# Bilinear bias in a deformable-attention kernel: left columns weighted by diagonal matrices on TensorE, and the right columns of one block in eight with them

## The chip, the cores and the metric

One Trainium2 chip, one of its cores. The metric is the device time of one execution in microseconds (us); three executions of the kernel before were timed. A profile of one more execution shows when each instruction ran on each engine: TensorE (PE), VectorE (DVE), ScalarE (ACT), GpSimd (POOL) and SyncE (SP, which issues DMAs).

## The reference, cut to what matters

Two layers: a deformable attention over 4 images of 32x32 pixels with 384 channels and 6 heads, then a linear attention and a mixture of four experts. The change lies in the first layer, where each head adds a bias to the attention logits. The bias of key n at all queries is a 32x32 window of a table, sampled bilinearly at an offset that belongs to that key:

```python
attn = jnp.einsum('bmhc,bnhc->bhmn', qh, k) * scale
disp = (ref.reshape(1, n, 1, 2) - pos.reshape(Bq * G, 1, n, 2)) * 0.5
...
bias = _bilinear_sample(rpe_img, disp)   # top = tl + ax*(tr - tl), bot likewise; top + ay*(bot - top)
...
attn = jax.nn.softmax(attn + bias, axis=-1)
out = jnp.einsum('bhmn,bnhc->bmhc', attn, v).reshape(Bq, Hq, Wq, NC)
return out @ w_out + b_out
```

## The kernel before, in words

The kernel has stages one after the other: normalisation, query projection, convolution, sampling of the keys and values (to about 400 us in the profile), the attention (to about 1395 us), the linear attention, and the experts. All data is float32. The attention stage is the one that the change touches.

Its loops run over 24 units (4 images x 6 heads) of 1024 keys and 1024 queries. A unit's keys are cut into 8 blocks of 128; two blocks make a pair `p`, so there are 96 pairs, and pair `p` is number `kp = p % 4` of its unit. Keys lie on the partitions, queries along the free axis. `e` (0 or 1) is the block within its pair.

For each block the bias is made in four steps with four weights per key, one number per partition (`weight(p, e, i)`, i = 0 to 3):
- `fetch_windows` (L1168): POOL fetches a 33x33 window of the table for each key by an indirect DMA into `win` (4 buffers).
- `upper` (L1184, ACT): rows 0 to 31 of the window times weight 0, into the tile `t` of 32x33 per key (4 buffers).
- `lower` (L1194, DVE): rows 1 to 32 times weight 1, added to `t`.
- `left` (L1202, ACT): columns 0 to 31 of `t` times weight 2, into the tile `o` of 32x32 per key (2 buffers). PE adds it to the logits in PSUM by a product with the identity (L1226, in `scores`).
- `right` (L1252, DVE): columns 1 to 32 of `t` times weight 3, plus the logits from PSUM, into the tile `S` in SBUF (6 buffers).

`scores(p, step)` makes the logits of a pair in the PSUM tile `ps`, of which there is one buffer (four banks of eight). PE's array is used as four quadrants of 64x64. In `step` 0 the products of queries and keys (L1221) go to the crossed quadrants for block 1, and the identity products of `o` (L1226) to the diagonal quadrants for block 0; in `step` 1 the blocks are exchanged. Each step has four products of each kind, each with 512 columns. Between the two steps PE waits for a small copy on ACT (`turn_over`, L1241).

After `right`, DVE keeps a running maximum over the pairs of a unit (`running`, L1270 and L1272). At the end of the unit PE transposes it (`highest`, L1282), DVE reduces it (L1286), and PE spreads the result (`spread`, L1298), which ACT copies (L1306). One unit later DVE subtracts it (`minus`, L1311), ACT takes the exponential (`weights_of`, L1315), and PE multiplies with the values (`values`, L1329 with the values and L1338 with ones). `out_of`, `to_queries` and `to_channels` (L1354 to L1412) finish a head, and `project` (L1429 to L1442) projects a finished image, 128 rows at a time. In the first units, where no image is finished, `last_pieces` runs what is left of the key and value projections of the stage before (helpers at L257 to L299).

The order on PE, ACT, DVE and POOL is that of the source. The loop at L1521 makes one turn per pair; turn `g` works on the scores of pair `g + 1` and on windows of pair `g + 2`, and finishes pairs four and five back:

```python
values(g - 5, 0)
scores(g + 1, 0)
for e in range(2):
    upper(g + 2, e)
...                                  # running(g), turn_over(g + 1), values(g - 5, 1), minus, weights_of
scores(g + 1, 1)
...                                  # highest, last_pieces(0), project(0)
for e in range(2):
    if kp:
        lower(g + 2, e)
    left(g + 2, e)
fetch_windows(g + 4)
right(g + 1)
```

Here `kp` is that of `g`, so the pair with number 3 is scored in the turn with `kp` = 2, and the maximum that takes it in stands in the turn with `kp` = 3, as does `highest`. `project` and `last_pieces` put their products behind `scores(g + 1, 1)` in turns with even `kp`.

Before the loop, L1504 to L1520 bring the first pairs in: four window fetches, `upper`, `lower`, `left`, `scores(0, ...)` and `right(0)`. The stage before ends with gathers of the sampled image (L871, POOL, six to a tile `ga`) that DVE weighs and adds (L886, L890, L891). Its PE, ACT, DVE and POOL work and that of the new stage share the engines' queues in one order, which follows when a tile's memory becomes free as well as the source.

Of the kernel before, what the change touches and what calls it, by code (L numbers as in the profile page):

```python
# [11 lines left out]
F32 = mybir.dt.float32  # L12
I32 = mybir.dt.int32
AF = mybir.ActivationFunctionType
# [5 lines left out]
P = 128  # L20
B, HI, WI, NC = 4, 32, 32, 384
# [3 lines left out]
G, GC = 6, 64  # L25
# [126 lines left out]
def bc(ap, axis, n):  # L152

    dims = [list(d) for d in ap.ap]
    dims.insert(axis, [0, n])
    return bass.AP(ap.tensor, ap.offset, dims)
# [3 lines left out]
def body(  # L160
# [8 lines left out]
    nc = tc.nc  # L169
# [11 lines left out]
    ident = const.tile([P, P], F32, tag="ident", name="ident")  # L181
# [60 lines left out]
    x0 = early.tile([P, NB, NC], F32, tag="x0", name="xr0")  # L242
# [58 lines left out]
    with tc.tile_pool(name="a_w", bufs=1) as aw, tc.tile_pool(name="a_1", bufs=1) as a1, tc.tile_pool(  # L301
        name="a_2", bufs=2
    ) as a2, tc.tile_pool(name="a_3", bufs=2) as a3, tc.tile_pool(name="a_s", bufs=2) as asm, tc.tile_pool(
        name="a_cv", bufs=1, space=PSUM
    ) as pcv, tc.tile_pool(name="a_mm", bufs=2, space=PSUM) as pmm, tc.tile_pool(
        name="a_tr", bufs=3, space=PSUM
# [13 lines left out]
        step = plan.step  # L320
# [379 lines left out]
        os_ = {}  # L700
# [222 lines left out]
        for b in range(B):  # L923
# [56 lines left out]
            for f in range(2):  # L980
# [22 lines left out]
                for i, n in enumerate(sizes):  # L1003
                    k0, r = K4 * f + i * n, n / K4
# [109 lines left out]

    with tc.tile_pool(name="b_w", bufs=1) as bwp, tc.tile_pool(name="b_qkv", bufs=2) as bq, tc.tile_pool(
        name="b_win", bufs=4
    ) as bwin, tc.tile_pool(name="b_t", bufs=4) as bt, tc.tile_pool(name="b_o", bufs=2) as bo_, tc.tile_pool(
        name="b_s", bufs=6
    ) as bS, tc.tile_pool(name="b_m", bufs=2) as bm, tc.tile_pool(name="b_ao", bufs=1) as bao, tc.tile_pool(
        name="b_y", bufs=3  # L1120
# [2 lines left out]
        nc.sync.dma_start(wo, w_out.rearrange("(a p) d -> p a d", p=P))  # L1123
        bo = bwp.tile([P, NC], F32, tag="bo", name="bo")
        nc.sync.dma_start(bo, bc(b_out, 0, P))
        units = [(b, h) for b in range(B) for h in range(G)]
        ao = {}
        heads = {}

        HALF = [slice(e * GC, (e + 1) * GC) for e in range(2)]  # L1130
        FULL = [slice(f * 512, (f + 1) * 512) for f in range(2)]
        SYNC = mybir.DependencyInfo(mybir.DependencyClass.Sync, mybir.DependencyReason.DATA)
        KP = NB // 2
        NP = KP * len(units)

        def load_qk(u):


            b, h = u
            c, r0 = h // 2, (h % 2) * GC  # L1140
            q = bq.tile([P, N], F32, tag="q", name=f"q{b}_{h}")
            k = bq.tile([P, NB, GC], F32, tag="k", name=f"k{b}_{h}")
            ks = k_d[b][c][r0 : r0 + GC, :].rearrange("p (a e j) -> p a e j", e=2, j=GC)
            for e in range(2):
                nc.sync.dma_start(q[HALF[e], :], q_d[b][c][r0 : r0 + GC, :])
                nc.sync.dma_start(k[HALF[e]], ks[:, :, 1 - e, :])
            return q, k
# [9 lines left out]


        wins, ts, os_, pss, Ss, turns = {}, {}, {}, {}, {}, {}
        qk, vs, ms, nms, pbss, pos, avs = {}, {}, {}, {}, {}, {}, {}  # L1160

        def fetch_windows(p):
# [13 lines left out]
        def weight(p, e, i):  # L1176
            b, h = units[p // KP]
            return bw[b][:, 2 * (p % KP) + e, h, i : i + 1]
# [19 lines left out]
        def left(p, e):  # L1198

            if p < NP:  # L1200
                o = bo_.tile([P, HI, WI], F32, tag="o", name=f"o{p}_{e}")
                nc.scalar.activation(o, ts[p, e][:, :, 0:WI], AF.Copy, scale=weight(p, e, 2))  # L1202
                os_[p, e] = o.rearrange("p y x -> p (y x)")

        def scores(p, step):


            if p >= NP:
                return
            i, kp = divmod(p, KP)  # L1210
            if step == 0:
                if kp == 0:
                    qk[i] = load_qk(units[i])
                pss[p] = bps.tile([P, 2, N], F32, tag="s", name=f"ps{p}")
            q, k = qk[i]
            ps = pss[p]
            e, d = 1 - step, step
            made = []
            for f in range(2):
                for r in range(2):  # L1220
                    made.append(nc.tensor.matmul(  # L1221
                        ps[HALF[1 - r], e, FULL[f]], k[HALF[r], 2 * kp + e, :], q[HALF[r], FULL[f]],
                        start=(step == 0), stop=(step == 1),
                    ))
                for r in range(2):
                    made.append(nc.tensor.matmul(  # L1226
                        ps[HALF[r], d, FULL[f]], ident[HALF[r], HALF[r]], os_[p, d][HALF[r], FULL[f]],
                        start=(step == 0), stop=(step == 1),
                    ))
            if step == 0:  # L1230
                turns[p] = made
            else:
                for i_ in made:
                    tc.add_manual_dep(i_.ins, turns[p].ins.name, SYNC, reason="second quarters")
                del turns[p]
# [10 lines left out]
        def right(p):  # L1246

            if p < NP:
                ps = pss.pop(p)
                st = bS.tile([P, 2, N], F32, tag="S", name=f"S{p}")  # L1250
                for e in range(2):
                    nc.vector.scalar_tensor_tensor(  # L1252
                        st[:, e, :].rearrange("p (y x) -> p y x", x=WI),
                        ts.pop((p, e))[:, :, 1:WIN],
                        weight(p, e, 3),
                        ps[:, e, :].rearrange("p (y x) -> p y x", x=WI),
                        ALU.mult,
                        ALU.add,
                    )
                    del os_[p, e]  # L1260
                Ss[p] = st
# [236 lines left out]
        with tc.manual_schedule(  # L1498
# [9 lines left out]
            for p in range(2):  # L1508
                for e in range(2):
                    upper(p, e)  # L1510
                    lower(p, e)
                    if p == 0:
                        left(p, e)
                fetch_windows(p + 2)
            scores(0, 0)
            turn_over(0)
            scores(0, 1)
            for e in range(2):
                left(1, e)
            right(0)  # L1520
            for g in range(NP + 7):  # L1521


                i, kp = divmod(g, KP)
# [4 lines that stand above are left out]
# [30 lines left out]
# [5 lines that stand above are left out]
                if kp % 2 == 0:  # L1564
                    project(1)
                right(g + 1)
                if g == 15 * KP:
                    load_early()
# [7 lines left out]
            while waiting:  # L1576
                tag, n = spots.pop(0)
# [152 lines left out]
    with tc.tile_pool(name="c_1", bufs=1) as c1, tc.tile_pool(name="c_2", bufs=2) as c2, tc.tile_pool(  # L1730
        name="c_s", bufs=2
# [320 lines left out]
    with tc.tile_pool(name="d_w1", bufs=1) as dw1, tc.tile_pool(name="d_s1", bufs=1) as ds1, tc.tile_pool(  # L2052
        name="d_w2", bufs=1
    ) as dw2, tc.tile_pool(name="d_s2", bufs=1) as ds2, tc.tile_pool(name="d_2", bufs=2) as d2p, tc.tile_pool(
        name="d_h", bufs=3
# [94 lines left out]
        for t in range(-2, len(units)):  # L2150
# [12 lines left out]
            d = ds[j]  # L2163
# [59 lines left out]
```

## Time and profile before

| | us |
|---|---|
| three runs | 2848.89, 2853.29, 2854.21 (median 2853.29) |
| the profiled execution | 2848.2 |
| its span | 2846.1 |
| PE busy, of the span | 2586.8 (91%) |
| DVE | 1579.4 (55%) |
| ACT | 1157.8 (41%) |
| POOL | 855.1 (30%) |
| mean granted TensorE clock | 0.968 of full speed |

| line, engine | count | mean us | busy us |
|---|---|---|---|
| L1226 PE, left columns by the identity | 1536 passes | 0.612 | 378.4 |
| L1221 PE, queries by keys | 1536 passes | 0.611 | 382.1 |
| L1184 ACT, `upper` | 192 | 1.168 | 218.1 |
| L1202 ACT, `left` | 192 | 1.144 | 212.8 |
| L1194 DVE, `lower` | 192 | 1.316 | 244.7 |
| L1252 DVE, `right` | 192 | 1.277 | 237.1 |
| L1306 ACT, copy of 128x1024 from PSUM | 24 | 0.993 | 23.8 |

How to read it: a busy share is an average over stages with different limits. One float32 product shows as two passes on PE, and passes in different quadrants run at the same time, so their durations overlap and their sum is no time on PE. In a list in order of time the columns are the start and the duration in us, the engine, the line, the operation, what is written and read, the shapes (partitions x elements) and the count; a bracket gives the idle time of the engine just before and what ended it.

### The profile page before, as it was taken

What the parts mean: (1) busy time and instruction counts of PE and PEld (TensorE: products, weight loads), DVE (VectorE), ACT (ScalarE), POOL (GpSimd) and SP (SyncE); (2) the same over time, 40 slices, a digit from 0 to 9 for tenths busy, and PEclk for the clock granted to TensorE, in tenths of its full rate; (3) what the DMA queues carried; (4) which work ended last, traced back from release to release, by engine and by line L of the source; (5) the groups of instructions that cost most, each with busy time, mean ns of one, the idle gap of its engine ahead of it and who ended that gap; (6) DMA issues with size and microseconds to landing.
All of it is one profiled execution on the core that took longest, in us unless ns stands there. A gap on an engine that the chain in (4) does not pass through costs nothing. (4 is left out here: it accounts for less than half of the span.)

```text
span 2846.1 us, 33342 instructions
## 1 busy us (share of the span) xinstructions
PE 2586.8 (91%) x12731; PEld 1283.8 (45%) x12731; DVE 1579.4 (55%) x2349; ACT 1157.8 (41%) x1532; POOL 855.1 (30%) x776
## 2 busy tenths in 40 slices
PE   8899938898989988888799898999999999999999
PEld 5455512332333333233365554555555555555566
DVE  3888859999999999999656765000101011011011
ACT  5565536777667766676323322111111111111121
POOL 1668863232333333332112335211112111021121
PEclk9899969999999999999999999999999999999999
DMA  7934575454546555544121312622223433374371
GB/s 205 257 114 132 175 208 165 130 154 146 164 145 195 176 157 149 145 151 127 55 74 51 120 45 70 250 103 103 103 103 118 147 129 140 115 255 172 117 267 59
DMA packets 267899, 404.77 MB, mean 142 GB/s; under 512 B 134674, under 2 KB 207634, under 8 KB 267356
## 3 DMA queue, kind: packets, MB, share of 16 engines
q1 hardware_dynamic: 214912, 230.43, 25.6%
q0 software_dynamic: 52112, 172.15, 18.7%
q8 instruction: 100, 1.64, 0.2%
q14 instruction: 59, 0.48, 0.1%
q10 hardware_dynamic: 716, 0.07, 0.0%
HBM read 345.68 MB, written 70.06 MB: 146 GB/s over the span
## 5 line engine op out<-in xcount | busy, mean ns | idle before, releaser
L2070 PE MATMUL ph<-d_xT,w 128*128 128x512 f32 (+1 forms) x1152 | 484.1, 554 | 1.3 <-ACT h L2077 1.3
L2102 PE MATMUL acc<-w,h 128*128 128x384 f32 x1392 | 480.3, 486 | 0.0
L1168 POOL DMA_INDIRECT win<-table,widx x192 | 280.2, 1459 | 640.3 <-DVE t L1194 608.5
L1221 PE MATMUL ps<-q,k 64*64 64x512 f32 x1536 | 382.1, 611 | 90.7 <-DVE S L1252 43.6
L2077 ACT ACTIVATE h<-ph,b1c 128x512 f32<-128x512 f32 (+1 forms) x192 | 124.1, 647 | 776.3 <-PE ph L2070 761.7
L1226 PE MATMUL ps<-o,ident 64*64 64x512 f32 x1536 | 378.4, 612 | 9.5 <-ACT o L1202 9.5
L2102 PEld LDWEIGHTS acc<-w,h 128*128 128x128 f32 x1392 | 264.1, 190 | 208.5 <-issue 73.2
L2070 PEld LDWEIGHTS ph<-d_xT,w 128*128 128x128 f32 x1152 | 217.0, 191 | 196.3 <-issue 144.5
L2132 POOL DMA_INDIRECT out<-rows,ei x67 | 67.1, 1002 | 700.2 <-DVE rows L2129 691.4
L871 POOL DMA_INDIRECT ga<-img,pidx x192 | 233.5, 1216 | 145.7 <-DVE gd L600 62.5
L1315 ACT ACTIVATE S<-S 128x2048 f32<-128x2048 f32 x96 | 183.4, 1910 | 190.3 <-DVE S L1311 190.3
L1221 PEld LDWEIGHTS ps<-q,k 64*64 64x64 f32 x1536 | 99.2, 134 | 355.4 <-issue 211.5
L1722 DVE COPY d_xT<-e_tr 128x512 f32<-128x512 f32 (+2 forms) x75 | 36.6, 512 | 386.1 <-PE e_tr L1719 386.1
L1194 DVE SCALAR_TENSOR_TENSOR t<-win,bw,t 128x1056 f32<-128x1056 f32 x192 | 244.7, 1316 | 5.9 <-ACT t L1184 4.6
L1252 DVE SCALAR_TENSOR_TENSOR S<-t,bw,ps 128x1024 f32<-128x1024 f32 x192 | 237.1, 1277 | 18.9 <-PE ps L1226 16.0
L2121 DVE SCALAR_TENSOR_TENSOR rows<-b2r,en,rows 128x384 f32<-128x384 f32 x67 | 40.9, 618 | 359.9 <-DMA rows<-out,ei 321.1
L1184 ACT ACTIVATE t<-win,bw 128x1056 f32<-128x1056 f32 x192 | 218.1, 1168 | 39.2 <-DMA win<-table,widx 38.1
L1202 ACT ACTIVATE o<-t,bw 128x1024 f32<-128x1024 f32 x192 | 212.8, 1144 | 37.0 <-DVE t L1194 30.1
L1329 PE MATMUL po<-S,v 128*64 128x512 f32 x768 | 199.1, 642 | 24.4 <-ACT av L1354 13.9
L1311 DVE TENSOR_TENSOR S<-S,pbs 128x2048 f32<-128x2048 f32 x96 | 219.0, 2283 | 2.1 <-ACT pbs L1306 2.1
L2129 DVE SCALAR_TENSOR_TENSOR rows<-acc,en,rows 128x384 f32<-128x384 f32 x67 | 41.4, 618 | 218.2 <-PE acc L2102 216.3
L1270 DVE TENSOR_TENSOR m<-m,S 128x2048 f32<-128x2048 f32 x48 | 117.1, 2440 | 1.6
(350 smaller groups left out, 3442.0 us busy)
## 6 DMA issues: line engine op xcount, KB each, us to landing
w<-in_L_ffn_w SPq DMA_DIRECT2D x50, 2304.0 KB
img<-in_x SPq DMA_DIRECT2D x48, 256.0 KB
q<-q_d SPq DMA_DIRECT2D x48, 256.0 KB
x<-in_x SPq DMA_DIRECT2D x8, 768.0 KB
q_d<-qt SPq DMA_DIRECT2D x24, 256.0 KB
v_d<-qkvw SPq DMA_DIRECT2D x32, 192.0 KB
v<-v_d SPq DMA_DIRECT2D x24, 256.0 KB
k<-k_d SPq DMA_DIRECT2D x48, 128.0 KB
```

The lines of the kernel that those rows point to most:

```text
L871: nc.gpsimd.indirect_dma_start(out=ga[:, g].rearrange("p s c -> p (s c)"), out_offset=None, in_=img[b][:, :], in_offset=bass.IndirectOffse ...
L1168: nc.gpsimd.indirect_dma_start(out=win, out_offset=None, in_=tables[h // 2][:, :], in_offset=bass.IndirectOffsetOnAxis(ap=widx[b][:, nb, h ...
L1184: nc.scalar.activation(t.rearrange("p y x -> p (y x)"), wins[p, e][:, : HI * WIN], AF.Copy, scale=weight(p, e, 0),)
L1194: nc.vector.scalar_tensor_tensor(tf, wins.pop((p, e))[:, WIN:], weight(p, e, 1), tf, ALU.mult, ALU.add)
L1202: nc.scalar.activation(o, ts[p, e][:, :, 0:WI], AF.Copy, scale=weight(p, e, 2))
L1221: made.append(nc.tensor.matmul(ps[HALF[1 - r], e, FULL[f]], k[HALF[r], 2 * kp + e, :], q[HALF[r], FULL[f]], start=(step == 0), stop=(step ...
L1226: made.append(nc.tensor.matmul(ps[HALF[r], d, FULL[f]], ident[HALF[r], HALF[r]], os_[p, d][HALF[r], FULL[f]], start=(step == 0), stop=(ste ...
L1252: nc.vector.scalar_tensor_tensor(st[:, e, :].rearrange("p (y x) -> p y x", x=WI), ts.pop((p, e))[:, :, 1:WIN], weight(p, e, 3), ps[:, e, : ...
L1311: nc.vector.tensor_tensor(Ss[p], Ss[p], bc(pbss[p // KP][:, :], 1, 2), ALU.add)
L1329: nc.tensor.matmul(pos[i][0][HALF[f], :], vs[i][:, 2 * kp + e, :], Ss[p][:, e, FULL[f]], start=(first and e == 0), stop=(last and e == 1),)
L2070: nc.tensor.matmul(ph if short(d) else ph[:, :n], a, m, start=(c == 0), stop=(c == CK - 1))
L2102: nc.tensor.matmul(d["acc"][0 if short(d) else s][:, :NC], h[:, s * P : (s + 1) * P], d["w2"][:, hc, :], start=(hc == 0), stop=(hc == HC - 1),
```

## The change

ACT no longer weighs the left columns of a block. It writes a diagonal instead: `fold` is a tile of two 64x64 identities one above the other, and `diagonal` multiplies it by the weight of each key, which gives a 128x64 tile. `scores` multiplies this tile with the columns of `t` themselves, read by rows of 32 out of 33, in the place of the product of the identity with `o`. The tile `o` is 64 wide and has 6 buffers in the place of 2. For one block in eight (pair 3 of each unit, block 1) a second diagonal is made from weight 3, `scores` adds the right columns in the same way behind the left ones, and `right` copies the finished logits of that block from PSUM to `S` on ACT in the place of the pass on DVE.

```diff
-    ) as bwin, tc.tile_pool(name="b_t", bufs=4) as bt, tc.tile_pool(name="b_o", bufs=2) as bo_, tc.tile_pool(
+    ) as bwin, tc.tile_pool(name="b_t", bufs=4) as bt, tc.tile_pool(name="b_o", bufs=6) as bo_, tc.tile_pool(
...
+        fold = bwp.tile([P, GC], F32, tag="fold", name="fold")
+        for e in range(2):
+            nc.gpsimd.tensor_copy(
+                fold[e * GC : (e + 1) * GC, :], ident[e * GC : (e + 1) * GC, e * GC : (e + 1) * GC]
+            )
...
+        WHOLE, rights = ((3, 1),), {}
...
             if p < NP:
-                o = bo_.tile([P, HI, WI], F32, tag="o", name=f"o{p}_{e}")
-                nc.scalar.activation(o, ts[p, e][:, :, 0:WI], AF.Copy, scale=weight(p, e, 2))
-                os_[p, e] = o.rearrange("p y x -> p (y x)")
+                os_[p, e] = diagonal(p, e, 2)
+                if (p % KP, e) in WHOLE:
+                    rights[p, e] = diagonal(p, e, 3)
+
+        def diagonal(p, e, i):
+            o = bo_.tile([P, GC], F32, tag="o", name=f"o{p}_{e}_{i}")
+            nc.scalar.activation(o, fold, AF.Copy, scale=weight(p, e, i))
+            return o
+
+        def columns_of(p, e, r, f, x0):
+
+            return ts[p, e][HALF[r], 16 * f : 16 * f + 16, x0 : x0 + WI]
...
                 for r in range(2):
                     made.append(nc.tensor.matmul(
-                        ps[HALF[r], d, FULL[f]], ident[HALF[r], HALF[r]], os_[p, d][HALF[r], FULL[f]],
-                        start=(step == 0), stop=(step == 1),
+                        ps[HALF[r], d, FULL[f]], os_[p, d][HALF[r], :], columns_of(p, d, r, f, 0),
+                        start=(step == 0), stop=(step == 1 and (p, d) not in rights),
+                    ))
+                for r in range(2 if (p, d) in rights else 0):
+                    made.append(nc.tensor.matmul(
+                        ps[HALF[r], d, FULL[f]], rights[p, d][HALF[r], :], columns_of(p, d, r, f, 1),
+                        start=False, stop=(step == 1),
                     ))
...
                 for e in range(2):
+                    if rights.pop((p, e), None) is not None:
+                        nc.scalar.copy(st[:, e, :], ps[:, e, :])
+                        del os_[p, e], ts[p, e]
+                        continue
                     nc.vector.scalar_tensor_tensor(
```

## The prediction

> **What bounds the kernel now.** I read the row of 40 slices first, then busy times over a stretch of the attention stage, then the groups of that stretch, then its instructions in order of time. The stage runs from about 400 to 1395 us. VectorE (DVE) is full there from the seventh slice to the nineteenth, and TensorE (PE) close to it. Over 900 us in the middle (columns: length, then busy us of PE, weight loads, DVE, ACT, POOL, the granted clock, DMA):
>
> ```profile
> PE   8899938898989988888799898999999999999999
> DVE  3888859999999999999656765000101011011011
> ...
> 440.00:1340.00 900.00, 791.80 (x5228) 282.16 (x5224) 872.53 (x623) 632.65 (x634) 284.98 (x202) 0.98 0.52 155
> ```
>
> DVE is busy 872.5 of 900 us (97%), PE 88%, ACT 70%; the clock was 0.98. An average does not say whether PE could take more, so I looked at the turn that the change loads. A unit (one image, one head) has four turns; the block pair with kp = 3 is scored in the turn kp = 2. Unit 9, and then unit 10, from that point on:
>
> ```profile
> 797.10 2.20 PE L1429 MATMUL y<-wo,ao 128*128 128x384 f32 x6
> 798.66 2.47 DVE L1252 SCALAR_TENSOR_TENSOR S<-t,bw,ps 128x1024 f32<-128x1024 f32 x2
> 799.24 1.94 PE L1329 MATMUL po<-S,v 128*64 128x512 f32 x8
> 801.16 2.82 DVE L1270 TENSOR_TENSOR m<-m,S 128x2048 f32<-128x2048 f32 x1
> 801.23 0.74 PE L1221 MATMUL ps<-q,k 64*64 64x512 f32 x2
> ...
> 806.10 1.09 PE L1282 MATMUL pm<-ident,m 128*128 128x128 f32 x8
> 807.82 1.22 DVE L1286 TENSOR_REDUCE nm<-pm 128x8 f32<-128x1024 f32 x1
> ```
>
> ```profile
> 836.02 2.20 PE L1429 MATMUL y<-wo,ao 128*128 128x384 f32 x6
> 838.49 1.94 PE L1329 MATMUL po<-S,v 128*64 128x512 f32 x8 [0.26 <-ACT S L1315]
> 838.86 2.47 DVE L1252 SCALAR_TENSOR_TENSOR S<-t,bw,ps 128x1024 f32<-128x1024 f32 x2
> ...
> 841.43 0.74 PE L1221 MATMUL ps<-q,k 64*64 64x512 f32 x2 [1.01 <-issue]
> 846.30 1.09 PE L1282 MATMUL pm<-ident,m 128*128 128x128 f32 x8
> 848.04 1.22 DVE L1286 TENSOR_REDUCE nm<-pm 128x8 f32<-128x1024 f32 x1
> ```
>
> In unit 9 the scores end at 797.17 (the last L1221/L1226 pair starts at 796.58 and takes 0.6), and PE then runs without a hole: projection, values to 801.18, the next scores at 801.23. DVE's pass over the old scores ended at 801.13, so both engines arrive together. Six us later DVE's reduction L1286 needs the transposes L1282, and they end at 807.19, 0.63 before it. In unit 10 PE has 0.26 + 1.01 us of holes before the next scores, then 0.65. The reduction is where the two meet: everything DVE does next stands behind it, so what it moves by is what the unit moves by.
>
> **The change part by part.** All sums are against the profiled execution: 2848.2 us, 2846.1 of it span. That lies 3.9 below the mean of the three runs (2852.1) and 5.1 below their median, 2853.29.
>
> *Left columns.* ACT's L1202 (192 × 1.144 = 219.6 us by its mean, 212.8 busy) becomes a 128x64 pass. Nothing of that size is in the trace; the nearest are L800's 128x48 at 0.24 and the token copy's 128x1 at 0.19, so 0.25, and bounds 0.19 to 0.47 (L295, 128x384). ACT is 70% busy and its waits there are for DVE, as these lines of the stretch 440 to 1340 show (busy, mean ns, idle before and its releaser):
>
> ```profile
> L1202 ACT ACTIVATE o<-t,bw 128x1024 f32<-128x1024 f32 x178 | 197.0, 1143 | 27.9 <-DVE t L1194 24.7
> L1306 ACT COPY pbs<-pb 128x1024 f32<-128x1024 f32 x23 | 22.8, 992 | 0.0
> ```
>
> What ACT issues next (L1184) waits for the tile that DVE's L1252 frees, so the saving ends as ACT idleness: 0. PE does the same count of 64x64 matmuls for the left columns, with rows of 32 out of 33. The convolution's L713 reads 32 of 34 and takes 0.375 for 256 columns against 0.589 for 512: 0.214 for 256 columns, the rate of plain rows. So 0 there too; if strided rows cost more, 1536 passes would pay it, but no row speaks for it.
>
> *Right columns of 24 blocks (p % 4 = 3, e = 1).* PE gets four more matmuls a block, each two passes in the trace (L1226: 1536 rows for 768 matmuls). They use the same two quadrants as the left ones, and passes in one quadrant follow at 0.43 (804.22, 804.70, 805.13, 805.56). The half-step's diagonal quadrants go from 4 passes to 8: +4 × 0.4275 = 1.71 us. Bounds: 0.86, if half of them slip into the stretch in which the other two quadrants work, and 1.95, a whole half-step. I take 1.71, because two passes of one quadrant have never overlapped in the trace. DVE loses one of its two passes: 2.47 becomes 1.28. ACT gets a copy from PSUM of the same shape as L1306: 0.99.
>
> *A new wait.* In the built program that copy waits for VectorE's instruction on the first half of the same tile, not for PE. So the two run one after the other: 1.28 + 0.03 (ACT's start after a DVE end at 401.41) + 0.99 + 0.10 (DVE after ACT at 399.99) = 2.40 against 2.47 + 0.03. Behind the copy, DVE's L1270 needs the tile and PE's next scores need the PSUM buffer, which has no second copy. DVE's 24 × 1.28 = 30.7 us thus come back as waiting, all but 0.1 a unit.
>
> *What 1.71 us more on PE do to each unit*, by the ends in the trace (hole of PE before the next scores, and gap between L1282's end and L1286):
> - Units 1, 3, 5, 11, 12: a late piece (L270, L286) and values fill PE, holes 0, gap 0.04: +1.71 each, 8.55.
> - Units 0 and 4: holes 0.2 to 0.3: +1.42 each, 2.84. Units 2 and 6: hole 1.0: +0.65 each, 1.3.
> - Units 7, 9, 13, 15, 19, 21: projection, and the transposes L1405 of an odd head before the half-step, holes 0 to 0.1, gap 0.63 to 0.66: 1.71 less 0.65, +1.0 to 1.1 each, 6.15.
> - Units 8, 10, 14, 16, 20, 22, also 18 and 23: holes and gap of 1.9 or more swallow it; −0.1 each, −0.8. Unit 17: +0.2.
>
> Sum +18.2. Of the delay nothing is won back: after the reduction DVE has no hole up to the next unit that it could close.
>
> *The start of the stage.* The order of the built program moves more than the diff shows. Three of the first four window fetches (L1168) now stand ahead of the last 24 gathers (L871) on POOL, and ACT's first L1184 ahead of key and value copies, so ACT and, behind it, DVE stop until the first window lands.
>
> ```profile
> 393.36 1.97 POOL L1168 DMA_INDIRECT win<-table,widx  x1 [0.30 <-issue]
> 402.64 1.12 PE L1226 MATMUL ps<-o,ident 64*64 64x512 f32 x2 [9.52 <-ACT o L1202]
> 412.07 2.47 DVE L1252 SCALAR_TENSOR_TENSOR S<-t,bw,ps 128x1024 f32<-128x1024 f32 x2 [2.23 <-PE ps L1226]
> ```
>
> The three fetches took 393.36 to 399.69 = 6.3, so the gathers' last data, in use at 396.8, come at 403.1. The small matrix `fold` waits for them on POOL, the diagonals for `fold`: 403.4. ACT's next L1184 ends at 404.9, and DVE then has in its order the leftovers of the sampling (0.96 + 0.61, twice, and 1.76) and three L1194 (1.32): 8.9, so the first L1252 starts at 413.8 and not at 412.07: +1.7. SP's loads of keys stand behind ACT's late copies: ACT's stop runs from 345.6 to 366.6 (a fetch issued at 360 lands 5.4 later, L1184 1.17), so the copies that ended at 360.7 end near 379; keys landed at 391.2 and land near 402.4, hidden, because PE waits for the diagonals until 403.7. Bounds −2 (the wait for PE at 412.07 gone) and +6.3 (the fetches in full). `fold` itself, two 64x64 copies, lies in this.
>
> Total: +18.2 + 1.7 = +19.9, so 2868.1 by the profiled execution, and 2872 with the 3.9 by which the runs' mean lies higher.
>
> A page speaks against my reading of PE: the Trainium skill, Perfetto Trace Analysis, section Identifying the Most-Contended Engine, says that matmul busy time is no good measure of TensorE's headroom and that the share of weight loads is. Weight loads are 31% of the stretch above, by which PE would have room for the four matmuls, their price would be 0 and the sum far lower. The rows of unit 9, where the next scores follow the values with no hole, do not agree, and I go by them.
>
> **Rivals.**
> - *Half price on PE* (0.86): units 1, 3, 5, 11, 12 +4.3, 0 and 4 +1.1, the six odd ones +1.2, the rest −1.1: +5.5 + 1.7 = 7.2, so 2859. For it: four quadrants do run at once. Against: left and right share a quadrant.
> - *Faster*: the copy runs beside DVE's first half after all, and the four matmuls are free. Then the nine units on whose path PE already stands gain 0, the six odd ones their gap of 0.65, the nine others 1.19: −14.6 + 1.7 = −12.9, so 2839. It decides only where PE's price is under some 0.3 a block and the wait named above is not as built. For it: DVE at 97%. Against: both rows and the program.
> - *The start costs all it can*: 18.2 + 6.3 = 24.5, so 2877; or more, if the gathers fall behind the key loads on the DMA queues, which are busiest there. For it: an ACT stop of 21 us. Against: PE had 9.52 us of waiting there to give.
>
> **How the numbers follow.** Forecast 0.64, start dearer 0.14, half price 0.14, faster 0.06, nothing measurable from other causes 0.02. Predicted 2872. The range goes from a little under the half-price case, 2853 (start at −2, rest as there), to 2885: 1.95 a block adds 0.24 × 15 units = 3.6, start +6.3, and the scatter of the runs, 5. What counts as a difference here is 0.2%, 5.7 us: up to 2859 is the same. Slower 0.84, same 0.10, faster 0.06.
>
> **What would show it.** In the changed profile: the second half-step of kp = 2 lasting 3.4 to 3.7 instead of 1.95; DVE's L1270 of kp = 3 waiting about 1.1 for ACT's copy, 24 times; the reduction waiting for L1282 by over 1 us in units with a piece or an odd projection; DVE's busy time some 30 us less and its idle time some 50 more; the spacing of L1286 near 41.8 instead of 41.0. I am wrong if the half-step grows by under 1 us, if the copy starts before DVE's half ends, or if the first L1252 begins outside 410 to 419.

## The result, and the profile after

The changed kernel takes 2881.34 us (median of 2879.92 to 2883.80), the kernel before 2853.75 on the same chip: +27.6 us, ratio 1.0095, 95% interval 1.0081 to 1.0109. The profiled execution took 2879.92 us, span 2878.2, 32.1 more than the span before. PE is busy 2626.7 us (+39.9), DVE 1550.3 (-29.1), ACT 1034.3 (-123.5).

Line numbers of the profile after differ: `upper` is L1192, `lower` L1202, the diagonals L1215, queries by keys L1238, left columns L1243, right columns on PE L1248, `right` on DVE L1278, the copy on ACT L1275, the running maximum L1296 and L1298, its transposes L1308, the reduction L1312. The row of 40 slices, for PE and DVE:

```profile
PE   8898748998899989888799898999999999999999
DVE  3788758899999899999647665010011011011011
```

DVE's row has 8s where it had 9s, and both engines are emptier in the fifth slice (288 to 360 us), ahead of the stage. The same stretch of 900 us as before, then groups of it (busy us, mean ns, idle time of the engine before them and what ended it):

```profile
440.00:1340.00 900.00, 805.74 (x5330) 283.08 (x5328) 831.55 (x590) 510.76 (x669) 279.97 (x198) 0.99 0.51 154
```

```profile
L1192 ACT ACTIVATE t<-win,bw 128x1056 f32<-128x1056 f32 x176 | 202.1, 1173 | 110.0 <-DVE S L1278 107.0
L1296 DVE TENSOR_TENSOR m<-m,S 128x2048 f32<-128x2048 f32 x44 | 106.1, 2411 | 25.6 <-ACT S L1275 24.9
L1312 DVE TENSOR_REDUCE nm<-pm 128x8 f32<-128x1024 f32 x22 | 26.9, 1223 | 25.3 <-PE pm L1308 25.3
L1275 ACT COPY S<-ps 128x1024 f32<-128x1024 f32 x22 | 22.3, 1012 | 34.9 <-DVE S L1278 34.9
```

DVE went from 872.5 to 831.6 us, PE from 791.8 to 805.7, and nothing got faster. ACT's saving became waiting, nearly all of it for DVE (L1192, 107.0 of 110.0 us). DVE waits 24.9 us for the new copy (22 times 1.13), and its reduction 25.3 us for PE's transposes, where the whole execution before had 10.2. Unit 11, in which PE had no hole before (in order of time, weight loads and POOL left out), first in the profile before:

```profile
875.66 0.65 PE L1221 MATMUL ps<-q,k 64*64 64x512 f32 x2
...
877.01 0.59 PE L1226 MATMUL ps<-o,ident 64*64 64x512 f32 x2
877.54 2.84 PE L270 MATMUL pl<-xT,qkvw 128*128 128x512 f32 x6
...
888.06 1.22 DVE L1286 TENSOR_REDUCE nm<-pm 128x8 f32<-128x1024 f32 x1 [0.71 <-PE pm L1282]
```

And in the changed kernel:

```profile
888.95 0.65 PE L1238 MATMUL ps<-q,k 64*64 64x512 f32 x2
...
890.73 1.02 PE L1243 MATMUL ps<-t,o 64*64 64x512 f32 x4
...
891.59 1.02 PE L1248 MATMUL ps<-t,o 64*64 64x512 f32 x4
...
892.54 2.84 PE L270 MATMUL pl<-xT,qkvw 128*128 128x512 f32 x6
892.66 1.28 DVE L1278 SCALAR_TENSOR_TENSOR S<-t,bw,ps 128x1024 f32<-128x1024 f32 x1 [0.20 <-PE ps L1248]
...
894.03 1.01 ACT L1275 COPY S<-ps 128x1024 f32<-128x1024 f32 x1 [1.59 <-DVE S L1278]
...
895.08 2.29 DVE L1296 TENSOR_TENSOR m<-m,S 128x2048 f32<-128x2048 f32 x1 [1.13 <-ACT S L1275]
...
901.94 1.09 PE L1308 MATMUL pm<-ident,m 128*128 128x128 f32 x8
903.07 1.23 DVE L1312 TENSOR_REDUCE nm<-pm 128x8 f32<-128x1024 f32 x1 [2.23 <-PE pm L1308]
```

The half-step lasts from 888.95 to 892.61, 3.66 us where 1.94 stood (875.66 to 877.60), and the piece L270 follows at once in both. DVE's half, the copy and the running maximum run one after the other, as forecast. DVE then idles 2.23 us ahead of the reduction, which starts 0.04 behind the transposes; it comes 1.72 later against before than that of unit 10 did.

Where the 32.1 us arise, as the lateness against the profile before at five points: +2.2 at 325 us, still in the stage before; +6.9 at the first reduction; +21.7 at the last; +28.7 at 1500 us, in the linear attention; +32.1 at the end. I count the 2.2 and the last 3.4 as no part of the change: the profiles of other kernels taken beside (below, on chips without the 40 us named there) have +1.0 to +4.1 and +1.9 to +4.0 in the same places, and the profile before is of an execution 5.5 us under its median. That leaves 4.7 for the start with unit 0, 14.8 for the other 23 units, and 7.0 for the stretch behind the stage: 26.5, beside 27.6 by the medians.

### The profile page after: what moved, and what is told of

Its sections match the earlier page's. It is cut to its first block, busy times and chain, and to the rows that moved or that the text cites. A ratio compares the mean times of both kernels' runs of the same rounds, so it can differ in the third digit from the quotient of the medians.

```text
span 2878.2 us, 33612 instructions
## 1 busy us (share of the span) xinstructions
PE 2626.7 (91%) x12923; PEld 1295.9 (45%) x12923; DVE 1550.3 (54%) x2325; ACT 1034.3 (36%) x1580; POOL 856.6 (30%) x778
## 5 line engine op out<-in xcount | busy, mean ns | idle before, releaser
L1238 PE MATMUL ps<-q,k 64*64 64x512 f32 x1536 | 381.7, 613 | 84.8 <-DVE S L1278 55.5
L1243 PE MATMUL ps<-t,o 64*64 64x512 f32 x1536 | 383.3, 613 | 2.6 <-ACT o L1215 2.6
L1192 ACT ACTIVATE t<-win,bw 128x1056 f32<-128x1056 f32 x192 | 220.7, 1173 | 142.6 <-DVE S L1278 120.7
L1202 DVE SCALAR_TENSOR_TENSOR t<-win,bw,t 128x1056 f32<-128x1056 f32 x192 | 245.0, 1315 | 21.1 <-ACT t L1192 19.9
L1238 PEld LDWEIGHTS ps<-q,k 64*64 64x64 f32 x1536 | 94.8, 134 | 348.5 <-issue 184.1
L1278 DVE SCALAR_TENSOR_TENSOR S<-t,bw,ps 128x1024 f32<-128x1024 f32 x168 | 208.4, 1276 | 21.2 <-PE ps L1243 11.5
L1355 PE MATMUL po<-S,v 128*64 128x512 f32 x768 | 188.7, 613 | 16.4 <-ACT av L1380 13.6
L1296 DVE TENSOR_TENSOR m<-m,S 128x2048 f32<-128x2048 f32 x48 | 115.9, 2414 | 27.9 <-ACT S L1275 27.1
L1881 POOL DMA_INDIRECT tab_d<-ent,si x64 | 65.4, 1022 | 163.6 <-DVE selw L1876 141.0
```

What stands on the lines that cost most here:

```text
L1192: nc.scalar.activation(t.rearrange("p y x -> p (y x)"), wins[p, e][:, : HI * WIN], AF.Copy, scale=weight(p, e, 0),)
L1202: nc.vector.scalar_tensor_tensor(tf, wins.pop((p, e))[:, WIN:], weight(p, e, 1), tf, ALU.mult, ALU.add)
L1238: made.append(nc.tensor.matmul(ps[HALF[1 - r], e, FULL[f]], k[HALF[r], 2 * kp + e, :], q[HALF[r], FULL[f]], start=(step == 0), stop=(step ...
L1243: made.append(nc.tensor.matmul(ps[HALF[r], d, FULL[f]], os_[p, d][HALF[r], :], columns_of(p, d, r, f, 0), start=(step == 0), stop=(step == ...
L1278: nc.vector.scalar_tensor_tensor(st[:, e, :].rearrange("p (y x) -> p y x", x=WI), ts.pop((p, e))[:, :, 1:WIN], weight(p, e, 3), ps[:, e, : ...
L1355: nc.tensor.matmul(pos[i][0][HALF[f], :], vs[i][:, 2 * kp + e, :], Ss[p][:, e, FULL[f]], start=(first and e == 0), stop=(last and e == 1),)
```

## The experiments

Twelve further kernels ran. On some of the chips every kernel, that of before too, took some 40 us longer, nearly all of it between 90 and 135 us of the profile. Ratios are therefore to the kernel before on the same chip, and of the profiles I use differences within a profile: from 325 us to the first reduction (start), from there to the last (units), and on to 1500 us (behind), each against the profile before.

| run | ratio to before, 95% | start | units | behind |
|---|---|---|---|---|
| the change | 1.0095 (1.0081 to 1.0109) | +4.7 | +14.8 | +7.0 |
| left_only | 1.0032 (1.0017 to 1.0047) | -3.1 | -0.7 | +6.7 |
| left_same | 0.9982 (0.9960 to 1.0004) | -5.9 | -1.2 | -1.1 |
| all_same | 1.0062 (1.0041 to 1.0083) | -5.2 | +14.1 | +1.9 |
| all_ps | 1.0018 (1.0002 to 1.0034) | -4.0 | +5.1 | +4.3 |
| copy_only | 0.9978 (0.9969 to 0.9987) | -4.8 | -2.8 | +4.2 |
| copy_only_ps | 0.9918 (0.9904 to 0.9931) | +0.6 | -20.2 | +1.5 |
| pad_o | 1.0045 (1.0029 to 1.0062) | +4.7 | +14.4 | -2.0 |
| fold_early | 1.0052 (1.0037 to 1.0066) | -2.2 | +13.5 | +5.5 |
| holes_ps | 0.9937 (0.9920 to 0.9954) | -7.3 | -10.0 | -2.3 |
| left_ps | 0.9981 (0.9963 to 0.9999) | -7.4 | -3.4 | -1.9 |
| moved_left | 1.0042 (1.0023 to 1.0060) | -5.1 | +14.1 | +2.1 |
| moved_ps | 1.0031 (1.0015 to 1.0047) | -2.2 | +15.1 | -1.7 |

From unit 2 on, single units repeat to some hundredths of a us between kernels that treat them alike, except where the granted clock differs. Unit 3, before and in the change:

```profile
537.35 3.08 PE L1329 MATMUL po<-S,v 128*64 128x512 f32 x8 [1.81 <-ACT av L1354]
```

```profile
547.39 1.94 PE L1355 MATMUL po<-S,v 128*64 128x512 f32 x8 [1.83 <-ACT av L1380]
```

The wait ahead is the same, but the clock granted from 538.0 to 541.4 us before was 0.50, and in the change it was 1.00 over its row. Over the whole of unit 3, before, left_only, left_same, all_ps and copy_only have a mean clock of 0.96 and the nine others 1.00. Without the passes for the right columns the unit takes 41.13 us at 0.96 and 39.53 at 1.00 (left_same, left_ps); with them 42.85 and 41.28 (all_ps, all_same). So the clock makes 1.6 us there and the passes 1.7. Units 18 and 19 differ between the kernels in the same way, by 1.1 to 1.6 us, again with a mean clock of 0.96 or 1.00, and unit 15 of left_same is 1.0 us longer at 0.92. Why the clock fell in one kernel and not in the next is not shown. A sum over the units carries such differences, and the starts and the stretch behind scatter by a few us.

### Rights or no rights, tiles as in the change or as before

left_only is the change without the right columns. In left_same and all_same the memory is laid out as before: two `o` tiles of 1024 columns, of which the diagonals take 64 or 128, and `fold` made at the start of the program.

```diff
# left_only, left_same
-        WHOLE, rights = ((3, 1),), {}
+        WHOLE, rights = (), {}
# left_same, all_same
+    fold = ab.tile([P, GC], F32, tag="fold", name="fold")     # beside token, with its two copies
-        name="b_o", bufs=6
+        name="b_o", bufs=2
+                o = bo_.tile([P, HI * WI], F32, tag="o", name=f"o{p}_{e}")
+                os_[p, e] = diagonal(p, e, 2, o[:, 0:GC])
+                    rights[p, e] = diagonal(p, e, 3, o[:, GC : 2 * GC])
```

> The change without the right columns on TensorE (no block has them, so no copy on ScalarE); fold and the small diagonal tiles as in the change. Theory (rights cost by their TensorE passes, the start and what follows the stage cost by where tiles lie in memory): the units 1 to 22 cost nothing, the start and the stretch after the stage cost 8 to 14 us, so about 2862 to 2868. Rival 1 (the left columns by diagonals cost by themselves in every pair): over 2870, spread over all units. Rival 2 (all of the loss comes from the rights): 2851 to 2856.

> The same without the right columns, but fold is made at the start of the program and the diagonals lie in two tiles as large as before, so that POOL's order is that of the kernel before. Theory: nothing is left of the loss, 2851 to 2857, first pass over the scores at 411 to 413 us, bn_stats after the stage within 1 us of before. Rival 1 (left columns cost): over 2860. Rival 3 (the late start comes from the diagonals, not from the memory): first pass over the scores at 415 or later.

> The whole change, with the tiles as large as before and fold early. Theory: only the 24 blocks with their right columns on TensorE cost, by 1.71 us where TensorE has no hole: +13 to +19 us, 2867 to 2873, and a spacing of the reductions that is that of the change. Rival 2 (all of the loss comes from the rights): 2878 to 2884. Rival 4 (rights cost under half of that and memory the rest): 2855 to 2862.

Measured: left_only +0.32%, with units of -0.7; left_same -0.18%, not to be told from no change; all_same +0.62%, some 18 us, with units of +14.1. So the left columns on diagonals cost nothing in the units (units 4, 6, 7 and 12 even gain 0.3, 1.1, 0.3 and 0.3 us in both kernels), and the right columns cost 15.3 us there (14.1 + 1.2). Where the tiles lie and when `fold` is made cost the rest: 0.5% between left_only and left_same, 0.33% between the change and all_same, by ratios. By ratios all three came out as the theory had it, left_only with 9 us near the lower end of its 8 to 14. Its profile bears out only half of that: +6.7 behind, but a start of -3.1.

### The copy freed from its wait

The copy on ACT waits for DVE because both read one PSUM tile; with a tile for each block the built program has it wait for PE alone. (The same edit divides the tile that the first transposes of the next stage take from this PSUM pool.)

```diff
-                pss[p] = bps.tile([P, 2, N], F32, tag="s", name=f"ps{p}")
+                pss[p] = [bps.tile([P, N], F32, tag=f"s{e}", name=f"ps{p}_{e}") for e in range(2)]
```

> As the run before it, with the logits of a pair in two PSUM tiles of one block each, so that the copy on ScalarE waits for TensorE alone and lies beside VectorE's pass on the other block. Theory (TensorE's passes are what costs): the wait of the running maximum for the copy goes from 1.1 to about 0, but units in which TensorE had no hole keep their price; 3 to 9 us less than with one tile, 2859 to 2868. Rival 5 (the copy's wait is what costs): 24 x 1.13 = 27 us less, 2840 to 2846. Rival 6 (the wait is wholly hidden): the same as with one tile within 2 us.

Measured: 1.0018, 0.44% or 13 us under all_same, with some 7 us either way by the two intervals (an estimate), and 8.9 us in the units. Unit 10 in order of time:

```profile
891.90 0.99 ACT L1275 COPY S<-ps 128x1024 f32<-128x1024 f32 x1
891.95 1.27 DVE L1278 SCALAR_TENSOR_TENSOR S<-t,bw,ps 128x1024 f32<-128x1024 f32 x1
...
893.33 2.29 DVE L1296 TENSOR_TENSOR m<-m,S 128x2048 f32<-128x2048 f32 x1
894.10 2.37 POOL L1464 TENSOR_TENSOR xk<-xk,bo 128x384 f32<-128x384 f32 x1
...
895.65 1.91 DVE L1298 TENSOR_TENSOR m<-m 128x1024 f32<-128x1024 f32 x1
```

The copy now lies beside DVE's pass and the maximum follows without a wait. Units 2, 6, 8, 10, 14, 16, 18, 20 and 22 gain 0.4 to 2.3 each against before, while 5, 11, 12, 13, 7, 9, 15 and 21 keep their loss to within 0.04 us. (Units 3 and 19, 1.6 slower and 1.6 faster than in all_same, differ by the clock.) So the wait cost in units where PE has room and was hidden behind PE in the others. 8.9 lies at the top of the 3 to 9 that the theory gave; 27, the wait in full, is excluded, and so is nothing.

### What PE's passes cost by themselves

copy_only and copy_only_ps are all_same and all_ps without the four matmuls.

```diff
-                for r in range(2 if (p, d) in rights else 0):
+                for r in range(0):
```

> As all_same (tiles as large as before, fold early), but TensorE leaves the right columns of the 24 blocks out: the third weight's part of the bias is missing there, while the second diagonal, the copy on ScalarE and its wait stay. What TensorE's passes cost is then the difference to all_same. Theory: from the first reduction to the last -1 to -4 us against before (the copy behind VectorE's pass takes 2.40 where two passes took 2.50, and the left columns gave -1.2), where all_same had +14.1; ratio to before 0.997 to 1.000. Rival (the copy's wait costs more than the passes): +5 us or more.

> The same with the logits in two PSUM tiles: no passes for the right columns (left out of the 24 blocks), and the copy beside VectorE's pass. Theory: what a block's right columns would bring if TensorE did them for nothing: 0.3 to 1.2 us a unit where VectorE is the bound, nothing where TensorE is: -8 to -20 us from the first reduction to the last; ratio 0.993 to 0.998. Rival (VectorE's time is worth nothing at all, since TensorE bounds every unit): as copy_only within 2 us.

Measured: copy_only -2.8 in the units and 0.9978. Against all_same the passes cost 16.9 us over 23 units, in which they are 23 x 1.71 = 39 us more of PE's time. Against left_same the copy behind DVE's pass gives 1.6, that is 0.07 a unit; 1.2 of it lies in units 15, 18 and 19, where the clock differs, so that some 0.4 is left (an estimate), 0.02 a unit. copy_only_ps gives -20.2 and 0.9918, a little more than expected: that is what DVE's saving is worth if the matmuls are free and the copy is not in its way. Groups of 440 to 1340 us, first of all_same, then copy_only, then copy_only_ps:

```profile
L1312 DVE TENSOR_REDUCE nm<-pm 128x8 f32<-128x1024 f32 x21 | 25.7, 1223 | 24.8 <-PE pm L1308 24.8
```

```profile
L1296 DVE TENSOR_TENSOR m<-m,S 128x2048 f32<-128x2048 f32 x44 | 109.7, 2493 | 24.5 <-ACT S L1275 23.7
L1312 DVE TENSOR_REDUCE nm<-pm 128x8 f32<-128x1024 f32 x23 | 28.1, 1221 | 11.4 <-PE pm L1308 11.4
```

```profile
L1296 DVE TENSOR_TENSOR m<-m,S 128x2048 f32<-128x2048 f32 x46 | 105.4, 2292 | 3.5 <-DVE S L1278 0.5
L1312 DVE TENSOR_REDUCE nm<-pm 128x8 f32<-128x1024 f32 x23 | 28.1, 1222 | 17.7 <-PE pm L1308 17.5
```

Without the passes the reduction's wait for PE falls from 24.8 to 11.4 us, near the 10.2 of before, while the wait ahead of the running maximum stays at 24.5, as in all_same: the passes, not the copy, are what made DVE late at the reduction. In copy_only_ps the copy's wait is gone, and PE, reached earlier, is waited for a little more.

### The start and the stretch behind the stage

pad_o is the change with `o` as large as before and `fold` where the change makes it; fold_early has the small `o` with six buffers and `fold` at the start of the program; each takes one half of the edit of all_same.

```diff
# pad_o: the change with
-        name="b_o", bufs=6
+        name="b_o", bufs=2
+                o = bo_.tile([P, HI * WI], F32, tag="o", name=f"o{p}_{e}")
# fold_early: the change with
-        fold = bwp.tile([P, GC], F32, tag="fold", name="fold")
+    fold = ab.tile([P, GC], F32, tag="fold", name="fold")
```

> The change with its diagonals in two tiles as large as the old ones, fold where the change makes it. Theory (two parts of the loss outside the units): the late fold and with it POOL's order cost the start, so the start is that of the change; the smaller o cost the stretch after the stage, so from the last reduction to the first layer norm of the next stage (1500 us) it is +1 to +3 against before, not +7. Rival: both come from fold, and the stretch after the stage still costs +7.

> The change with fold made at the start of the program and the small o of six buffers. Theory: the start is that of all_same (first pass over the scores 3 to 6 us earlier in its stage than in the change), the stretch after the stage costs +7 as in the change. Rival: the other way round.

Both came out on the theory's side, pad_o with -2.0 behind below its +1 to +3. The late `fold` costs at the start: +4.7 with it (pad_o), -2.2 without (fold_early), 6.9 us on the same chip. How much is not settled: two other kernels with the early `fold` have -4.8 and +0.6 on that chip, and left_only, with the late one, has -3.1 on a chip where three kernels with the early one have -4.0 to -5.9, so 1 to 3 us there. The change, around its start:

```profile
397.14 2.33 POOL L871 DMA_INDIRECT ga<-img,pidx  x1 [0.30 <-issue]
399.47 0.26 POOL L1129 COPY fold<-ident 64x64 f32<-64x64 f32 x1
406.26 0.23 POOL L1129 COPY fold<-ident 64x64 f32<-64x64 f32 x1 [6.54 <-DMA ga<-img,pidx]
...
406.53 0.35 ACT L1215 ACTIVATE o<-fold,bw 128x64 f32<-128x64 f32 x1 [26.86 <-POOL fold L1129]
406.79 1.16 ACT L1192 ACTIVATE t<-win,bw 128x1056 f32<-128x1056 f32 x1
...
416.38 2.47 DVE L1278 SCALAR_TENSOR_TENSOR S<-t,bw,ps 128x1024 f32<-128x1024 f32 x2
```

The second copy of `fold` waits on POOL for the last gather's data at 406.2, ACT's diagonal for it, the window pass for the diagonal and DVE for that. left_only has the same chain (its copy waits 6.87 us for the gathers). With `fold` early the first pass over the scores starts at 411.06.

The small `o` goes with the loss behind: +7.0, +6.7 and +5.5 in the three kernels that have it, -2.3 to +4.3 in the ten that don't. What is seen of it is that `bqs`, three numbers per partition for the next stage, moves into DVE's layer norm. The change, then pad_o:

```profile
1415.50 0.17 DVE L223 TENSOR_SCALAR c_lnr_a<-c_lnmv 128x8 f32<-128x8 f32 x1
1417.52 0.17 DVE L1769 TENSOR_SCALAR bqs<-cols 128x3 f32<-128x3 f32 x1 [1.85 <-PE po L1364]
1417.60 0.20 DVE L226 RECIPROCAL c_lnr_r<-c_lnr_r 128x8 f32<-128x8 f32 x1
```

```profile
1383.26 0.17 DVE L1769 TENSOR_SCALAR bqs<-cols 128x3 f32<-128x3 f32 x1
...
1414.02 0.17 DVE L223 TENSOR_SCALAR c_lnr_a<-c_lnmv 128x8 f32<-128x8 f32 x1
1414.46 0.20 DVE L226 RECIPROCAL c_lnr_r<-c_lnr_r 128x8 f32<-128x8 f32 x1 [0.28 <-ACT c_lnr_r L225]
```

In the change `bqs` waits until PE has read the last exponentials, and the chain from L223 to L226 takes 2.10 us instead of 0.44. That is 1.7 of the 7; the granted clock of 1420 to 1440 us, 0.74 against 1.00 in pad_o, goes with more of it. From the last reduction to 1500 us before, and to the same place in the others, the mean clock is 0.96 before, in left_same and in pad_o, and 0.92, 0.93 and 0.92 in the change, left_only and fold_early. But copy_only and all_ps, whose `o` is large, lose 4.2 and 4.3 there at 0.92 and 0.94. So beyond the 1.7 the small `o` is not shown to be the cause, and a lower clock for another reason is an open rival. Which tile's place makes which part was not tried: fold_early loses 5.5 with `bqs` waiting only 0.21. Nor do the ratios show that the two parts add: either half alone (1.0045 and 1.0052) comes out no worse than both together (all_same, 1.0041 to 1.0083); only the profiles do.

### Versions that might be faster

If PE's holes decide, the right columns should go only where there are any. holes_ps is all_ps with them in eleven units, and left_ps, without them anywhere, is its control.

```diff
-                if (p % KP, e) in WHOLE:
+                if (p % KP, e) in WHOLE and p // KP in (2, 6, 8, 10, 14, 16, 17, 18, 19, 20, 22):
```

> Two PSUM tiles, tiles as large as before, fold early, and the right columns on TensorE only in the eleven units 2, 6, 8, 10, 14, 16 to 20 and 22, where all_ps gained against left_same. Theory (the four matmuls are free where TensorE has a hole that takes them and VectorE is the bound): the gains of those units add, -8 to -11 us from the first reduction to the last, ratio 0.995 to 0.999. Rival (a unit's hole is only an echo of the delay in the unit before it, so that without that delay there is no gain): -1 to -3 us, as left_same.

> No right columns on TensorE, but the logits of a pair in two PSUM tiles: what the split gives by itself, and so what of the gain of holes_ps is owed to the right columns. Theory (the split only matters where ScalarE copies one of the two blocks): -1 to -2 us from the first reduction to the last, as left_same, so that 8 to 9 of the 10 us of holes_ps come from its eleven blocks; ratio 0.997 to 1.000. Rival (the split itself lets VectorE start early): -8 us or more, ratio 0.994 to 0.997.

Measured: holes_ps 0.9937 (0.9920 to 0.9954), units -10.0; left_ps 0.9981, units -3.4, more than expected. holes_ps is faster than both kernels. The units of holes_ps gain 6.6 us against left_ps, and left_ps gains 2.2 against left_same, but both differences carry the clock. left_ps has unit 18 at 0.96 and loses 1.2 there, which leaves some 5.4 us for the eleven blocks, less than the 8 to 9 that I gave them. Of the 2.2, units 3, 15 and 18 (-1.6, -1.0, +1.2) go with the clock, which leaves some 0.8 for the split tile (both are estimates from the spacings of the reductions). Units 8, 10, 16, 20 and 22 gain 0.5 each, 6 and 14 1.1 to 1.2, while unit 19 loses 1.0 and should be left out: I had picked it because all_ps gained 0.6 there, and that gain was the clock, 1.00 in all_ps against 0.96 before and in holes_ps.

PE also waits 1.88 us for DVE in most turns with kp = 0, ahead of the next scores. moved_left and moved_ps put the projection or the late piece there, and with it the copy of the spread maximum ahead of ACT's window passes.

```diff
                 values(g - 5, 0)
+                if kp == 0:
+                    spread(i - 1, 1)
+                    last_pieces(0)
+                    project(0)
                 scores(g + 1, 0)
...
                 if kp == 0:
-                    spread(i - 1, 1)
...
-                if kp % 2 == 0:
+                if kp == 2:
                     last_pieces(0)
                     project(0)
```

> left_same (no right columns on TensorE) with one move: in turns with kp = 0 the projection or the late piece goes to PE ahead of the first half-step of the next scores, where PE waits 1.88 us for VectorE, and ScalarE's copy of the spread maximum goes ahead of the window passes so that the PSUM tile is free. Theory (the units with a piece are bound by TensorE in this turn): -5 to -15 us from the first reduction to the last. Rival (VectorE is the bound at 97% and takes nothing): 0 to -3 us.

> all_ps (right columns of one block in eight on TensorE, two PSUM tiles) with the same move. Theory (the matmuls cost because TensorE has no room in the units with a piece; 1.88 us of room a unit pay for their 1.71): all_ps had +5 us from the first reduction to the last; now -10 to -20, ratio 0.991 to 0.997. Rival (the room is not on TensorE's path): within 3 us of all_ps.

Both missed, and by the sign: 1.0042 and 1.0031, units +14.1 and +15.1. The hole in left_same, and what came of it in moved_left:

```profile
890.27 0.65 PE L1238 MATMUL ps<-q,k 64*64 64x512 f32 x2 [1.88 <-DVE S L1278]
```

```profile
892.86 2.20 PE L1455 MATMUL y<-wo,ao 128*128 128x384 f32 x6
...
902.03 3.40 PE L1355 MATMUL po<-S,v 128*64 128x512 f32 x8 [2.22 <-ACT av L1380]
```

In its old place the piece had covered PE's wait for ACT's copy of the finished head (`av`) ahead of the next values. Moved away, it uncovers that wait: PE's idle time ahead of L1355 in 480 to 1400 us goes from 19.9 us in left_same to 47.5 (the part for `av` from 11.4 to 34.0). In the row above, the eight products behind the wait also took 3.40 us instead of 1.94, at a granted clock of 0.56 (902 to 905 us). The hole was there, but the piece already hid another of its size. The edit moves the copy of the spread maximum too, and what that does by itself was not tried.

## Why the prediction was right, point by point

- **Verdict.** Slower was forecast with 0.84, and 2872 in 2853 to 2885; measured 2881.34. The sum was +19.9 and the change costs +27.6. Direction and mechanism were right, and the sum was short by 6.6 us of the 26.5 that the profile shows: 1.6 at the start, 7.0 behind the stage, less 2.0 that the units cost under their forecast.
- **Left columns, 0.** Right: ACT's saving is idle time, the strided products take 0.613 us a pass against 0.612, and left_same is at 0.9982 with an interval that holds 1. That units 4, 6, 7 and 12 gain 2.0 us together was not in the forecast.
- **Right columns, 1.71 a block, only where PE has no hole.** Right: the half-step takes 3.66 instead of 1.95. For units 1 to 22 the forecast by units adds to 16.9, and the change shows 13.2; units 5 and 11 have 1.72, 12 has 1.41, 7, 9, 13, 15, 19 and 21 have 0.8 to 1.1, and 8, 10, 14, 16, 20 and 22 are within 0.02 of nothing. Unit 12 paid 1.72 as well, less the 0.3 of the left columns. Unit 3 shows 0.15 instead of 1.71: it paid its price and had 1.6 back by a granted clock of 1.00 where 0.96 stood before. Wrong in single units: 1 (2.70 instead of 1.71), 6 (-1.25 instead of 0.65, of which -1.1 is in left_same too) and 23 (1.55 instead of -0.1); their causes stay open. That errors of up to 1.9 us in one unit leave only 2.0 in the sum is partly luck. The mean spacing of the reductions grew by 0.64 us, from 40.30 to 40.94, where 0.8, from 41.0 to 41.8, was forecast. The prediction said that two passes of one quadrant never overlap; the rows show them 0.59 long and 0.43 apart, so they do overlap there. Its price rests on the spacing, and that held.
- **The new wait takes back DVE's saving, all but 0.1 a unit.** Right: 1.13 us, 24 times, and 0.07 a unit in copy_only, or 0.02 without the units in which the clock differs. The reading that two PSUM readers share one tile was not in the prediction; it had seen the wait in the program and not its reason.
- **The start, +1.7.** The chain was as forecast, `fold` behind the gathers and the windows behind `fold`, and its size nearly so. The gathers' last data, put at 403.1, came at 406.2, but 2.2 us of that stood at 325 us already. The rest of the chain took 8.4 us from ACT's L1192, not 8.9, so the first pass over the scores began at 416.38 where 413.8 was forecast and 412.07 stood before: +2.1 without the 2.2, against +1.7. Unit 0 was later still, +4.7 to the first reduction where 3.1 was forecast (the 1.7 and its 1.42); the clock granted between 420 and 430 was 0.78 there (before: 1.00), which goes with it.
- **Behind the stage, nothing.** This is the step that failed: the sum had no such term, and it is 7.0 us. The prediction looked at what the smaller `o` and `fold` move ahead of the stage and not at what they move behind it, though both come from the same program order. What the runs show in its place is 1.7 us by the later `bqs`, and a lower granted clock that goes with the rest; its cause stays open.
- **The rivals.** Half price is excluded by the half-step. The faster case needed two things at once, and the runs part them: the copy freed with the passes paid is +5.1 in the units, both together -20.2. The dear start (2877) was nearest in size, but only a quarter of the 6.6 us that the sum lacked lay there.

The page that spoke against the reading of PE, the Trainium skill's Perfetto Trace Analysis, section Identifying the Most-Contended Engine, judges TensorE's room by the share of weight loads and, beside it, by MFU (the share of the peak matmul rate), which was not worked out here. The share of weight loads is 31% before and after, and yet 1.71 us more work on PE in each of 23 units cost 16.9 us. Neither that share nor the busy share (88%) tells it; the holes of single units tell most of it.

## What to carry to other kernels

When two engines are both nearly full, price a move unit by unit by the holes of the engine that receives it; a mean share hides that the same four matmuls cost 1.7 us in one unit and nothing in the next. Look at who else reads a tile before giving one reader to another engine, since two readers of one PSUM tile can be put in a row by the program. A smaller or later scratch tile can move what lies around it in memory, so compare the built order behind a stage as well as ahead of it. Before reading a difference of 1 to 2 us in one unit as the edit's, compare the granted clock over that unit in both profiles.

## What was not expected of the hardware

VectorE and GpSimd got in each other's way: where POOL's bias addition L1464 (1.01 us alone) fell beside DVE's L1298 (1.23 alone), as in the rows of all_ps above, they took 2.37 and 1.91 us. From 893.33 the three operations are through at 897.56, 4.23 us, where 2.29 + 1.01 + 1.23 in a row are 4.53. The Trainium skill, Trainium Architecture — The Big Picture, section What this means for kernel authors, says of this pair's shared port that it is locked and not split; that nearly the whole sum shows agrees. L1296, which ran first, kept its 2.29. A copy that finishes earlier can move DVE into such a meeting: L1298 takes 1.9 us five times in all_ps, five times in holes_ps and eleven times in copy_only_ps, and never before or in all_same.

The granted clock was not a matter of the wait alone: eight products behind a wait of 1.81 us took 3.08 us before (0.50 from 538.0 to 541.4 us), and behind one of 1.83 us in the change 1.94.
